# One core, four graph layers: the hand-written list of steps is replaced by another list

## The chip, the core and the metric

The kernel runs on one core of a Trainium2 chip. The metric is the device time in microseconds (us) of one execution, the median of three runs. The engines that matter are TensorE (PE; its weight loads are shown apart as PEld), VectorE (DVE), ScalarE (ACT), GpSimd (POOL), and SyncE (SP), which issues the DMAs. "L2252" is line 2252 of the kernel.

## The reference, cut to what matters

128 graphs of 64 nodes with 128 features each; `adj` holds edge weights, about a quarter of them nonzero. Four layers, each added to `x` after a layer norm and a ReLU:

```python
h = relu(layernorm(x))                       # layer 0: filters made from edge lengths
g = exp(coeff * (adj[..., None] - offsets) ** 2)             # 64 Gaussians an edge
Wf = (softplus(g @ W1.T + b1) - log 2) @ W2.T + b2           # a filter of 128 an edge
x = x + mlp(sum_j (h @ Wa.T)[j] * Wf[i, j] * adj[i, j] ** 2)  # mlp with softplus
h = relu(layernorm(x))                       # layer 1: hyperbolic attention
p = proj(mobius_add(mobius_matvec(W, h), expmap0(b)))
loc = logmap(p[i], p[j]);  self = logmap(p, p)
att = sigmoid(silu([self, loc] @ att_w1.T + att_b1) @ att_w2.T + att_b2)
s = sum_j att * loc * adj
u = silu([self, s] @ mlp_w1.T + mlp_b1) @ mlp_w2.T + mlp_b2 + self
x = x + proj(expmap0(silu(logmap0(proj(expmap(u, p))))))
h = relu(layernorm(x));  x = x + (d * adj * d) @ h @ W + b   # layer 2: degree norm
h = relu(layernorm(x));  x = x + [h, mean_message(h)] @ W_upd # layer 3
```

## The kernel before, in words

**Tiling.** `sparse_stack` does all the work that the given inputs need: 16 groups of 8 graphs. The partitions hold two graphs of 64 nodes, and a group is 4 such pairs (indices 0 to 3), so a node tile is 128 x (4 x 128). Work per edge goes only over edges that exist: each node's neighbours are sorted into slots, and the slots lie in three blocks c = 0, 1, 2 of 512, 494 and 208 columns a pair (`BLOCKS`, `WIDTHS`). A name such as `filter_of13` is block 1, pair 3; blocks 0 and 1 go by single pairs or by two (pairs 0-1 and 2-3, written 0 and 2), block 2 too.

**Streams.** The work of a group is written as generators, called streams. `load` brings x and adj (DMAs L1419 and L1420), `order` sorts the neighbours into one-hot tiles `oh` (L1533, on DVE), and `normed_x` makes layer 0's normed input (POOL L1470 and L1472, ACT L1478 and L1486). Layer 0's edges are done by four kinds:

- `weights_of` (DVE) spreads edge lengths over slots; `squares` (ACT L1588) squares them.
- `duo` (PE L1599, ACT L1604 and L1607) makes the Gaussians.
- `filter_of` has these steps: w1T matmul (PE L1621), Exp (ACT L1628), Ln (ACT L1631), w2T matmul (PE L1638), product (DVE L1643), and sums over slots (DVE L1401 and others).
- `neighbours` (PE L1679, ACT copy L1685) brings the neighbours' features, which L1643 also reads.

`layer1_nodes` does layer 1's node part, many tiny DVE, ACT and POOL operations; L1819 (ACT) and L1823 (DVE) are two of them, and `product_with_bias` (POOL L1805, then a DVE reduction) belongs to it. Layer 1's edges are done by `coefs_of` (DVE L1387 spreads; later L2076 merges the attention), `rows` (PE L2096, DVE L2099), `scores_of` (PE L2114 and L2118, ACT Silu L2123), `heads` (PE L2140, ACT Tanh L2146 into the tile `row`, then four DMAs L2151 that copy `row` into `th`) and `no_scores` (a POOL memset, L2157). `coefs_of`'s L2076 waits for these row copies. `rest1` ends layer 1; the steps needed here, by number, are:

- 8: the two hid matmuls L2217 and L2218; 9: Silu L2220
- 10 and 11: a matmul, and the add L2226, which makes u
- 12: squares of u, L1289 with four accumulator reads (ACT)
- 13: floor and power on POOL (L1279, L1275)
- 14: L2249 and L2250 (DVE); 15: Tanh L2252 (ACT); 16 and on: L2254, L2257 and more (DVE).

`product_with_h` (POOL L2234, DVE L2239) runs beside them. `rest2` is layers 2 and 3, ending with the output's DMA (L2421); L1256 is its product with adj, L2341 a POOL addition in it, and L2403 ACT scalings. L1242, L1249 and L1209 are helpers (matmul by pairs or by graph, PSUM copies).

**Order.** Each `yield on(engine, ...)` begins a step and names its engine, the buffer rings it takes, the events it needs, and where it matters the activation table ("log" or "silu") that ACT must have. The list `ORDER` (from line 775) fixes the order of all steps: a token `name@-4` runs the next step of that stream of group it-4, and `name@=2` runs a step of a stream that is there once (weights and constants) in iteration 2. The whole list is gone through for it = -6 to 21; one pass holds a step of every stage, for several groups at once. PE, DVE, ACT and POOL are under a manual schedule: each of them executes exactly in the order in which the list issues its instructions. SP's DMAs are issued by the steps that contain them. A step that names a table issues a table load if the last step in the list that named one named the other:

```python
        _, takes, _, table = s.want
        if table not in (None, self.table):
            self.table = table
            self.scalar.preload_act_table_set({"log": "natural_log_exp_and_others",
                                               "silu": "silu_and_others"}[table])
```

It is line 925. Steps on PE name tables too: `filter_of`'s first step (w1T matmul) names "log", and `rest1`'s step 8 (hid matmuls) and `scores_of`'s first step name "silu", so that the load is issued ahead of the activation that needs it:

```python
            yield on(PE, "big", "ex", table="log")      # filter_of, step 0
        yield on(PE, "sm", table="silu")                # rest1, step 8: hid matmuls
        yield on(ACT, table="silu")                     # rest1, step 9: act(hid, pt, AF.Silu, ...)
```

Of the kernel before, what the change touches and what calls it, by code (L numbers as in the profile page):

```python
# [772 lines left out]

PE, DVE, ACT, POOL = "PE", "DVE", "ACT", "POOL"
ORDER = """
scores_of03@-4 sum_of_both@-5 layer1_nodes@-3 turned_from5@=2 heads02@-4 rows12@-4 scores_of10@-4
scores_of11@-4 turned_from3@=-1 layer1_nodes@-3 rest1@-5 coefs_of00@-4 rest1@-5 rest1@-5
coefs_of20@-4 rest1@-5 order@-2 rest1@-5 layer1_nodes@-3 layer1_edges@-4 rest1@-5 order@-2
heads02@-4 layer1_nodes@-3 scores_of10@-4 scores_of11@-4 rest1@-5 coefs_of00@-4 rest1@-5 rows12@-4
rest1@-5 rest1@-5 order@-2 rest1@-5 order@-2 layer1_nodes@-3 coefs_of00@-4 rest1@-5 layer0@-2  # L780
rest1@-5 coefs_of02@-4 rest1@-5 rest1@-5 weights0@=-2 weights_of00@-2 rest1@-5 turned_from5@=2
rest1@-5 rest1@-5 coefs_of02@-4 scores_of12@-4 layer1_nodes@-3 heads10@-4 duo00@-2 scores_of13@-4
rest1@-5 rest1@-5 coefs_of00@-4 rest1@-5 coefs_of02@-4 rest1@-5 layer1_nodes@-3 rest1@-5 rest1@-5
layer1_nodes@-3 rest1@-5 turned_from3@=-1 sum_of_both@-5 coefs_of02@-4 weights_of02@-2
scores_of12@-4 heads10@-4 squares00@-2 duo00@-2 scores_of13@-4 weights1@=0 rest1@-5 rest1@-5
layer1_nodes@-3 rest1@-5 rows20@-4 rows22@-4 heads12@-4 heads12@-4 squares02@-2 rest1@-5 rows22@-4
layer1_nodes@-3 layer1_nodes@-3 rows20@-4 weights2@=2 coefs_of10@-4 rest1@-5 rest1@-5 rest1@-5
rest1@-5 rest2@-5 coefs_of10@-4 scores_of22@-4 layer1_nodes@-3 scores_of20@-4 scores_of22@-4
layer1_nodes@-3 norm_of_h1@-3 layer1_nodes@-3 duo02@-2 root_of_sums@-5 rest2@-5 layer1_nodes@-3
scores_of20@-4 layer1_nodes@-3 coefs_of12@-4 coefs_of10@-4 weights_of10@-2 coefs_of10@-4  # L790
weights_of12@-2 coefs_of12@-4 weights0@=1 layer1_nodes@-3 rest2@-5 coefs_of12@-4 weights_of20@-2
heads20@-4 heads20@-4 duo00@-2 rest2@-5 rest2@-5 weights2@=3 layer1_nodes@-3 duo02@-2 rest2@-5
rest2@-5 product_with_bias@-3 coefs_of12@-4 layer1_nodes@-3 coefs_of20@-4 turned_from0@=-4
filter_of00@-2 neighbours00@-2 filter_of01@-2 weights2@=2 layer1_nodes@-3 filter_of00@-2
filter_of00@-2 duo02@-2 neighbours00@-2 filter_of01@-2 layer1_edges@-4 coefs_of20@-4
layer1_nodes@-3 layer1_edges@-4 layer1_nodes@-3 layer1_edges@-4 layer1_nodes@-3 layer1_nodes@-3
rest1@-4 layer1_nodes@-3 layer1_nodes@-3 rest1@-4 layer1_nodes@-3 layer1_nodes@-3 rest1@-4
layer1_nodes@-3 neighbours01@-2 rest2@-5 filter_of02@-2 rest1@-4 filter_of00@-2 layer1_nodes@-3
neighbours01@-2 filter_of02@-2 squares10@-2 filter_of01@-2 filter_of02@-2 layer1_nodes@-3
product_with_bias@-3 layer0@-2 layer1_nodes@-3 layer1_nodes@-3 rest2@-5 layer1_nodes@-3  # L800
weights2@=2 layer1_nodes@-3 layer1_nodes@-3 layer1_nodes@-3 layer1_nodes@-3 order@-1
layer1_nodes@-3 rest1@-4 layer1_nodes@-3 layer1_nodes@-3 rest1@-4 layer1_nodes@-3 layer1_nodes@-3
rest2@-5 layer1_nodes@-3 layer1_nodes@-3 layer1_nodes@-3 layer1_nodes@-3 turned_from0@=-3
layer1_nodes@-3 layer1_nodes@-3 filter_of00@-2 layer1_nodes@-3 layer1_nodes@-3 layer1_nodes@-3
layer1_nodes@-3 layer1_nodes@-3 layer1_nodes@-3 layer1_nodes@-3 layer1_nodes@-3 norm_of_sum@-3
duo20@-2 neighbours02@-2 rest2@-5 filter_of01@-2 rest2@-5 filter_of00@-2 order@-1 weights2@=3
filter_of00@-2 filter_of01@-2 norm_of_sum@-3 rest2@-5 neighbours02@-2 duo20@-2 layer1_nodes@-3
duo20@-2 rest2@-5 norm_of_sum@-3 filter_of00@-2 layer1_nodes@-3 layer1_nodes@-3 layer1_nodes@-3
order@-1 rest2@-5 filter_of01@-2 filter_of03@-2 neighbours03@-2 turned_from1@=-4 rest1@-4
turned_from2@=-1 layer1_nodes@-3 weights0@=0 weights0@=1 filter_of03@-2 neighbours03@-2  # L810
squares20@-2 layer1_nodes@-3 filter_of03@-2 layer1_nodes@-3 rest1@-4 weights0@=-1 filter_of02@-2
norm_of_h@-3 x_self@-4 rest2@-5 filter_of02@-2 filter_of01@-2 norm_of_h@-3 turned_from2@=-1
filter_of01@-2 slots_ranks@=0 duo22@-2 layer1_nodes@-3 filter_of20@-2 neighbours20@-2 duo22@-2
layer1_nodes@-3 duo22@-2 filter_of20@-2 neighbours20@-2 layer1_nodes@-3 filter_of02@-2
layer1_nodes@-3 filter_of02@-2 filter_of02@-2 layer1_nodes@-3 weights0@=-1 filter_of20@-2
layer1_nodes@-3 filter_of22@-2 order@-1 weights0@=-1 attention@-3 filter_of03@-2 weights0@=1
order@-1 layer1_nodes@-3 order@-1 rest2@-5 layer1_nodes@-3 layer1_nodes@-3 order@-1
layer1_nodes@-3 filter_of03@-2 attention@-3 filter_of22@-2 layer1_nodes@-3 attention@-3
weights0@=-2 duo10@-2 order@-1 filter_of20@-2 neighbours22@-2 one_minus_z@-3 rest2@-5
one_minus_z@-3 slots_ranks@=-6 layer1_nodes@-3 one_minus_z@-3 one_minus_z@-3 filter_of03@-2  # L820
weights0@=-1 rest2@-5 rest2@-5 attention@-3 duo10@-2 layer1_nodes@-3 one_minus_z@-3 duo10@-2
rest2@-5 neighbours22@-2 order@-1 layer1_nodes@-3 filter_of20@-2 weights0@=0 layer1_nodes@-3
order@-1 layer1_nodes@-3 filter_of03@-2 layer1_nodes@-3 layer1_nodes@-3 filter_of03@-2
filter_of20@-2 layer1_nodes@-3 layer1_nodes@-3 layer1_nodes@-3 layer1_nodes@-3 layer1_nodes@-3
layer1_nodes@-3 layer1_nodes@-3 order@-1 weights0@=0 duo12@-2 filter_of10@-2 filter_of11@-2
weights2@=2 rest2@-5 order@-1 duo12@-2 filter_of10@-2 filter_of22@-2 rest2@-5 filter_of11@-2
filter_of10@-2 layer1_nodes@-3 neighbours10@-2 order@-1 filter_of22@-2 rest2@-5 filter_of10@-2
order@-1 neighbours10@-2 rest2@-5 rest2@-5 filter_of22@-2 weights2@=2 layer1_nodes@-3 order@-1
slots_ranks@=-2 filter_of22@-2 filter_of10@-2 duo12@-2 layer1_nodes@-3 filter_of11@-2 rest2@-5
rest2@-5 neighbours11@-2 filter_of12@-2 filter_of11@-2 order@-1 layer1_nodes@-3 layer1_nodes@-3  # L830
weights1@=-6 filter_of10@-2 layer1_nodes@-3 neighbours11@-2 filter_of12@-2 squares12@-2 rest2@-5
filter_of10@-2 layer1_nodes@-3 turned_from1@=-2 filter_of10@-2 layer1_edges@-3 coefs_of00@-3
filter_of10@-2 filter_of11@-2 order@-1 coefs_of02@-3 rest2@-5 filter_of11@-2 order@-1 order@-1
filter_of13@-2 neighbours13@-2 neighbours12@-2 rest2@-5 filter_of12@-2 filter_of13@-2
neighbours13@-2 neighbours12@-2 filter_of13@-2 rows00@-3 filter_of12@-2 turned_from4@=1
filter_of13@-2 rest1@-4 weights0@=1 weights2@=2 rest2@-5 rows00@-3 filter_of12@-2 filter_of11@-2
filter_of12@-2 filter_of11@-2 filter_of13@-2 filter_of12@-2 filter_of13@-2 filter_of12@-2
filter_of11@-2 filter_of13@-2 load@0 filter_of12@-2 rest1@-4 weights1@=-3 rows02@-3 rest1@-4
scores_of01@-3 scores_of00@-3 rest1@-4 filter_of13@-2 layer0@-2 rows02@-3 filter_of13@-2
weights0@=1 layer0@-2 normed_x@-1 rest1@-4 scores_of01@-3 scores_of00@-3 product_with_h@-4  # L840
rest1@-4 normed_x@-1 normed_x@-1 no_scores@-3 normed_x@-1 sums_of_columns@-1 product_with_h@-4
weights0@=-2 turned_from4@=1 coefs_of10@-3 product_with_h@-4 rest1@-4 order@-1 scores_of02@-3
heads00@-3 rows10@-3 normed_x@-1 scores_of03@-3 scores_of02@-3 rest1@-4 heads00@-3 normed_x@-1
rest1@-4 rest1@-4 rest1@-4 weights2@=2 rest1@-4 rest1@-4 rest1@-4 weights1@=1 rest1@-4 rest1@-4
rest1@-4 order@-1 rest1@-4 order@-1 rest1@-4 rest1@-4 rest1@-4 coefs_of12@-3 rows10@-3 rest1@-4
normed_x@-1 normed_x@-1
"""


def elements(ap):  # L850
    n = 1
    for d in ap.shape[1:]:
        n *= d
    return n


# [1617 lines left out]
```

## Time and profile before

| | us |
|---|---|
| median of the runs shown | 1792.26 (1792.07 to 1797.98) |
| the profiled execution's own time | 1792.99 |
| its span in the trace | 1791.2 |
| PE busy | 1558.6 (87%), 10231 matmuls |
| DVE busy | 1570.0 (88%), 5020 instructions |
| ACT busy | 1447.4 (81%), 2756 instructions |
| POOL busy | 422.6 (24%), 718 instructions |
| one ACT table load (L925), 64 of them | 1.283 |

Read it so: three engines are busy over 80% of the span, and the chain of waits (the page's fourth part) divides itself among them: PE 29%, ACT 29%, DVE 28%. The granted TensorE clock is 0.937 on average. The same stage comes again at equal distance: L2252 starts at 998.1, 1100.7, 1203.4 and 1306.0, so a period, one pass through the list, is 102.6 us, and about 13 such periods lie between the filling of the pipeline (to about 181) and its emptying (from about 1511).

### The profile page before, as it was taken

What the parts mean: (1) busy time and instruction counts of PE and PEld (TensorE: products, weight loads), DVE (VectorE), ACT (ScalarE), POOL (GpSimd) and SP (SyncE); (2) the same over time, 40 slices, a digit from 0 to 9 for tenths busy, and PEclk for the clock granted to TensorE, in tenths of its full rate; (3) what the DMA queues carried; (4) which work ended last, traced back from release to release, by engine and by line L of the source; (5) the groups of instructions that cost most, each with busy time, mean ns of one, the idle gap of its engine ahead of it and who ended that gap; (6) DMA issues with size and microseconds to landing.
All of it is one profiled execution on the core that took longest, in us unless ns stands there. A gap on an engine that the chain in (4) does not pass through costs nothing.

```text
span 1791.2 us, 30395 instructions
## 1 busy us (share of the span) xinstructions
PE 1558.6 (87%) x10231; PEld 848.9 (47%) x10231; DVE 1570.0 (88%) x5020; ACT 1447.4 (81%) x2756; POOL 422.6 (24%) x718
## 2 busy tenths in 40 slices
PE   3959898998989899898989899898989989896853
PEld 2424444544545454454545454454545445454442
DVE  5559899999999999999999989999999999987843
ACT  2858897979798897979899797979889797986632
POOL 2010213223221413223121322312141322302221
PEclk8979999999999999999999999999999999997965
DMA  2000202010110202011020201011020201102110
GB/s 62 6 1 7 57 7 54 10 45 22 27 45 16 57 7 56 16 33 33 16 57 10 63 7 44 22 28 45 16 57 1 56 11 30 33 13 51 39 30 9
DMA packets 57174, 53.64 MB, mean 30 GB/s; under 512 B 13616, under 2 KB 48816, under 8 KB 57008
## 3 DMA queue, kind: packets, MB, share of 16 engines
q1 hardware_dynamic: 57008, 51.60, 11.9%
q8 instruction: 83, 1.36, 0.3%
q14 instruction: 83, 0.68, 0.1%
HBM read 7.61 MB, written 4.19 MB: 7 GB/s over the span
## 4 chain that ended last, share of the span: by engine, by line
PE 29%; ACT 29%; DVE 28%; issue 5%; DMA 4%; POOL 3%; SPq 1%; DVEq 0%; ACTq 0%; POOLq 0%
PE big L1638 7%; PE sm L1242 6%; DVE ex L1643 4%; DMA th<-row 4%; PE big L1621 3%; PE big L1679 3%; ACT ex L1628 3%; DVE va L1387 3%; ACT ra L1685 2%; ACT e L1607 2%; ACT e L1604 2%; ACT ex L1631 2%; ACT v L1284 2%; PE sm L1249 2%; ACT n L1209 2%
## 5 line engine op out<-in xcount | busy, mean ns | idle before, releaser
L1638 PE MATMUL big<-ex,w2T 128*128 128x512 f32 (+2 forms) x768 | 295.2, 517 | 14.8 <-DVE den L1723 11.8
L1643 DVE SCALAR_TENSOR_TENSOR ex<-big,c_L_gnn_b,ra 128x1024 f32<-128x1024 f32 (+2 forms) x160 | 195.8, 1224 | 31.9 <-PE big L1638 31.2
L1621 PE MATMUL big<-e,w1T 64*128 64x512 f32 (+2 forms) x768 | 182.3, 572 | 15.9 <-ACT e L1607 8.0
L2114 PE MATMUL big<-va,U 64*128 64x512 f32 (+2 forms) x768 | 174.6, 530 | 19.4 <-DVE va L2099 19.3
L1638 PEld LDWEIGHTS big<-ex,w2T 128*128 128x128 f32 x768 | 134.3, 190 | 116.1 <-issue 75.5
L1628 ACT ACTIVATE ex<-big,c_L_gnn_b 128x1024 f32<-128x1024 f32 (+2 forms) x160 | 175.8, 1099 | 3.9 <-PE big L1621 1.8
L2123 ACT ACTIVATE ex<-big,c_L_gnn_att_b 128x1024 f32<-128x1024 f32 (+2 forms) x160 | 165.8, 1068 | 15.5 <-PE big L2118 10.7
L1679 PE MATMUL big<-va,a 64*128 64x512 f32 (+2 forms) x768 | 173.5, 551 | 3.8 <-ACT va L1588 1.6
L1685 ACT ACTIVATE ra<-big 128x1024 f32<-128x1024 f32 (+2 forms) x160 | 159.0, 1015 | 11.0 <-DVE den L1723 8.1
L1631 ACT ACTIVATE ex<-ex 128x1024 f32<-128x1024 f32 (+2 forms) x160 | 166.8, 1055 | 0.5
L2118 PE MATMUL big<-slot_r,Sx 64*128 64x512 f32 (+2 forms) x768 | 164.4, 502 | 0.0
L2234 POOL TENSOR_TENSOR w<-w,hh 128x512 f32<-128x512 f32 x16 | 20.6, 1287 | 592.8 <-DVE w L2226 578.4
L1401 DVE TENSOR_TENSOR ex<-ex 128x512 f32<-128x512 f32 (+3 forms) x256 | 121.2, 483 | 0.2
L2076 DVE COPY_PREDICATED att<-oh,th 128x256 f32<-128x256 uint16 (+1 forms) x256 | 109.3, 443 | 12.9 <-DMA th<-row 12.2
L2096 PE MATMUL big<-oh,pqs 64*64 64x512 bf16 (+2 forms) x1152 | 113.3, 333 | 0.0
L1621 PEld LDWEIGHTS big<-e,w1T 64*128 64x128 f32 x768 | 68.9, 203 | 87.6 <-issue 31.0
L2140 PE MATMUL sm<-ex,aw2b 128*32 128x512 f32 (+2 forms) x640 | 93.6, 583 | 12.5 <-ACT ex L2123 11.2
L2099 DVE COPY_PREDICATED va<-slot_r,big 128x1024 f32<-128x1024 uint32 (+2 forms) x96 | 102.2, 1066 | 1.6 <-PE big L2096 1.6
L1679 PEld LDWEIGHTS big<-va,a 64*128 64x128 f32 x768 | 69.7, 196 | 70.2 <-issue 31.1
L2118 PEld LDWEIGHTS big<-slot_r,Sx 64*128 64x128 f32 x768 | 73.9, 187 | 58.5 <-issue 58.5
L2114 PEld LDWEIGHTS big<-va,U 64*128 64x128 f32 x768 | 63.0, 185 | 69.1 <-DVE va L2099 38.2
L1256 PE MATMUL big<-adjT,v 64*128 64x64 f32 x256 | 31.5, 420 | 72.2 <-ACT v L1284 72.2
(571 smaller groups left out, 3717.0 us busy)
## 6 DMA issues: line engine op xcount, KB each, us to landing
th<-row SPq DMA_DIRECT2D x64, 256.0 KB, 3.5
th<-row SPq DMA_DIRECT2D x64, 247.0 KB, 3.4
th<-row SPq DMA_DIRECT2D x64, 104.0 KB, 2.3
x<-in_x_dram SPq DMA_DIRECT2D x16, 256.0 KB, 2.9
out_dram<-v SPq DMA_DIRECT2D x16, 256.0 KB, 2.3
adj<-in_adj_dram SPq DMA_DIRECT2D x16, 128.0 KB, 2.3
e<-in_L_gnn_att_w_dram SPq DMA_DIRECT2D x2, 64.0 KB, 4.2
bR<-in_L_gnn_mlp_w_dram SPq DMA_DIRECT2D x2, 64.0 KB, 3.2
```

Source lines behind the costliest of these rows:

```text
L1401: V.tensor_tensor(dst, a[:, :, 0:n], a[:, :, n:2 * n], ALU.add)
L1621: T.matmul(dst, lhsT=w1T[HALF[h], :], rhs=e[HALF[h], b, 0:W], start=True, stop=True)
L1628: act(ex[:, :, 0:wide], pre[:, :, 0:wide], AF.Exp, bias=b1)
L1631: act(ex[:, :, 0:wide], ex[:, :, 0:wide], AF.Ln, bias=1.0)
L1638: T.matmul(wf[:, b, cols], lhsT=w2T, rhs=ex[:, b if c < 2 else b ^ j, cols], start=True, stop=True)
L1643: V.scalar_tensor_tensor(ex[:, :, 0:wide] if c < 2 else two.rearrange("q (j r) -> q j r", j=2), wf[:, :, 0:wide], b2s, ra[:, :, 0:wide], A ...
L1679: T.matmul(nb[:, b, at * W:at * W + W], lhsT=rf[rows, p + j, :], rhs=factors[0][rows, k + j, :], start=True, stop=True)
L1685: act(ra[:, :, 0:wide], nb[:, :, 0:wide], AF.Copy)
L2096: T.matmul(rk[h, k, 0:W], lhsT=pqs[h, s, p, :], rhs=oh[h, p, at:at + W], start=s == 0, stop=s == 2)
L2114: T.matmul(pre[:, b, col], lhsT=U[h, p + k, :], rhs=coefs[h, k, :], start=True, stop=False)
L2118: T.matmul(pre[:, b, col], lhsT=Sx[s][h, p + k, :], rhs=slot_r[h, at:at + W], start=False, stop=s == 1)
L2123: act(a[:, :, 0:wide], pre[:, :, 0:wide], AF.Silu, bias=ab1)
```

## The change

Only the string `ORDER` is replaced; everything else of the kernel is the same. The new list begins about half a pass later in the cycle than the old one (so the offsets of the stages behind that point differ by one), and within the cycle many steps have changed places with their neighbours. `load` stands about half a pass later in relation to the rest. The same instructions are issued on PE, DVE (5020) and POOL (718), each in a somewhat different order, and SP's DMAs come in the same order, line by line. On ACT the activations are the same, and table loads are 92 where they were 64. Of the places that are spoken of below, the old and the new list (steps of one pass, step number after the dot, steps of no matter left out):

```
old: ... filter_of13.1 neighbours13.1 neighbours12.1 filter_of13.2 rows00.0 filter_of12.3 filter_of13.3 rest1.8 ...
new: ... rest1.8 rest2.30 filter_of13.0 neighbours12.0 neighbours13.0 filter_of13.1 filter_of12.2 neighbours12.1 filter_of13.2 ... rest1.9

old: rest1.14 order.19 scores_of02.0 heads00.0 rows10.0 normed_x.4 scores_of03.0 scores_of02.1 rest1.15 heads00.1 normed_x.5 rest1.16
new: order.18 order.19 rest2.31 filter_of11.6 rows00.1 ... rest1.14 scores_of02.0 heads00.0 scores_of03.0 normed_x.4 rows10.0 rest1.15 heads00.1 normed_x.5 rest1.16 ... scores_of02.1 scores_of03.1

old: no_scores between normed_x.2 (L1470) and normed_x.3 (L1472);  new: ahead of product_with_h.0 (L2234)
old: coefs_of00's first merge (L2076) behind rest1.30;              new: behind rest1.33
old: product_with_bias.0 (L1805) behind rest2.6 (L2341);            new: ahead of it
```

The lines of the diff in which these stand:

```diff
 ORDER = """
...
-filter_of13@-2 neighbours13@-2 neighbours12@-2 rest2@-5 filter_of12@-2 filter_of13@-2
-neighbours13@-2 neighbours12@-2 filter_of13@-2 rows00@-3 filter_of12@-2 turned_from4@=1
-filter_of13@-2 rest1@-4 weights0@=1 weights2@=2 rest2@-5 rows00@-3 filter_of12@-2 filter_of11@-2
...
-rest1@-4 normed_x@-1 normed_x@-1 no_scores@-3 normed_x@-1 sums_of_columns@-1 product_with_h@-4
-weights0@=-2 turned_from4@=1 coefs_of10@-3 product_with_h@-4 rest1@-4 order@-1 scores_of02@-3
-heads00@-3 rows10@-3 normed_x@-1 scores_of03@-3 scores_of02@-3 rest1@-4 heads00@-3 normed_x@-1
...
+coefs_of00@-3 rest2@-5 filter_of11@-2 filter_of10@-2 rest1@-4 rest2@-5 filter_of13@-2
+neighbours12@-2 neighbours13@-2 filter_of13@-2 filter_of12@-2 neighbours12@-2 filter_of13@-2
+neighbours13@-2 rows00@-3 filter_of12@-2 filter_of13@-2 filter_of11@-2 order@-1 weights2@=2
+layer0@-2 coefs_of02@-3 order@-1 order@-1 rest2@-5 filter_of11@-2 rows00@-3 filter_of12@-2
...
+layer0@-2 normed_x@-1 rest1@-4 scores_of00@-3 scores_of01@-3 no_scores@-3 product_with_h@-4
+rest1@-4 normed_x@-1 normed_x@-1 normed_x@-1 product_with_h@-4 coefs_of10@-3 product_with_h@-4
+rest1@-4 scores_of02@-3 turned_from4@=1 heads00@-3 turned_from0@=-4 turned_from1@=-3
+scores_of03@-3 normed_x@-1 rows10@-3 rest1@-4 heads00@-3 normed_x@-1 rest1@-4 rest1@-4 rest1@-4
...
```

## The prediction

> **What bounds the kernel now.** The chain of waits of the whole run names no engine (PE 29%, ACT 29%, DVE 28%), so I cut one period at the places where the limit changes hands. The first view is busy time by windows (columns: window, length, busy us and count of PE, PEld, DVE, ACT, POOL, then clock, DMA share, GB/s):
>
> ```profile
> 283.00:1511.00 1228.00, 1138.65 (x7658) 618.95 (x7654) 1157.05 (x3706) 1079.47 (x2065) 314.54 (x516) 0.97 0.13 31
> 1074.60:1100.80 26.20, 26.09 (x153) 12.94 (x153) 26.06 (x55) 17.38 (x30) 6.57 (x9) 1.00 0.06 16
> 1100.80:1177.20 76.40, 68.23 (x491) 38.53 (x488) 70.17 (x256) 72.52 (x144) 19.77 (x35) 0.96 0.15 37
> ```
>
> The period of 102.6 us has two parts. For 26.2 us (from filter_of10's w2T matmul to L2252) PE and DVE are full and ACT has 8.8 us to spare. For 76.4 us ACT is the fullest, 72.5. So the first part is set by PE and DVE, the second mostly by ACT; work added to an engine in its own part costs, in the other part it does not.
>
> The second view is what ACT waited for in 283 to 1511, about 12 periods (us in total, times, longest); then the same for DVE:
>
> ```profile
> ACT w L2220 <- PE sm L2218: 44.3, 12, 3.7
> ACT w L1289 <- DVE w L2226: 32.7, 12, 2.7
> ACT a L1486 <- POOL d_n L1705: 15.7, 12, 1.3
> ACT ra L1685 <- DVE den L1723: 8.1, 12, 1.0
> ```
>
> ```profile
> DVE ex L1643 <- PE big L1638: 13.9, 24, 0.7
> DVE s L1823 <- ACT nn L1819: 12.0, 12, 1.1
> DVE e L1963 <- ACT gr L1209: 8.2, 12, 0.7
> DVE att L2076 <- DMA th<-row: 6.3, 12, 1.3
> ```
>
> ACT's two long waits (3.7 and 2.7 a period) lie in the first part, where it has slack. L1486 (1.31 a period) and L1685 (0.68) lie in the second, where they lengthen the period. Row copies cost DVE 6.3 us in 12 periods, 0.5 in each: all that a better guess at landing times could win directly. L1486 really waits for a matmul's result and L1685 for PE's buffer, which DVE's L1643 frees; the POOL and DVE rows named had long been done.
>
> The third view is the timeline where the first part ends (start, length, engine, line), of ACT, DVE and POOL:
>
> ```profile
> 1085.57 1.28 ACT L925 ACT_TABLE_LOAD   x1
> 1090.54 0.69 ACT L2220 ACTIVATE w<-sm,c_L_gnn_mlp_b 128x512 f32<-128x512 f32 x1 [3.69 <-PE sm L2218]
> 1095.14 3.20 ACT L2123 ACTIVATE ex<-big,c_L_gnn_att_b 128x1024 f32<-128x1024 f32 x3
> 1100.73 0.20 ACT L2252 ACTIVATE k__11817<-rb 128x4 f32<-128x4 f32 x1 [2.39 <-DVE rb L2249]
> ```
>
> ```profile
> 1099.16 0.17 DVE L2239 RECIPROCAL rb<-rb 128x4 f32<-128x4 f32 x1
> 1099.42 1.28 DVE L2249 TENSOR_TENSOR rb<-rb,un 128x4 f32<-128x4 f32 x1
> 1100.62 0.17 DVE L2250 RECIPROCAL ur<-un 128x4 f32<-128x4 f32 x1
> 1100.71 0.35 DVE L1533 TENSOR_TENSOR oh<-pos,slot_k 128x440 bf16<-128x440 bf16 x1
> ```
>
> ```profile
> 1097.91 1.07 POOL L1470 TENSOR_TENSOR a<-xp,o_mv 128x512 f32<-128x512 f32 x1
> 1098.93 0.52 POOL L2157 MEMSET att<- 128x512 f32 x1
> 1099.41 1.27 POOL L1472 TENSOR_TENSOR xp<-xp,r_L_gnn_bd 128x512 f32<-128x512 f32 x1
> ```
>
> L2249 does 512 numbers, as its neighbours of 0.17 do, yet is on record for 1.28: it ends (1100.70) when POOL's L1472 ends (1100.68). The Trainium skill, "SBUF — State Buffer", section "Who interferes with whom", has this as a port that the two engines share and that the first to issue holds for its whole instruction; the trace agrees (0.163 at the shortest, 1.275 in the median of this line's 16).
>
> **The change, part by part.** One period, in us; a plus is longer.
>
> *Table loads.* 92 for 64, two more in each steady pass: hid's matmul step (silu) now comes before filter_of13's first step (log), hid's Silu after it, so ACT loads silu, log and silu. Two loads of 1.283 are 2.57. They fall into the first part, where ACT idles 3.69 ahead of L2220. In exchange hid's matmuls no longer come last: PE has them 8.65 us of matmuls earlier, and L2220 then waits for its own third load, not for PE. ACT's last Ln before it ended at 1085.56; with 2.57 more and the third load it would be free at about 1089.4, before L2220's present 1090.54. Value 0. If the cover goes (ACT late for w2T of filter_of12 or filter_of13, where I find 2.3 spare: 1.41 from Ln's end at 1085.56 to the matmul at 1086.97, plus the 1.72 of PE work now ahead of it, less 0.83 of ACT shift), it costs at most 0.3. One place for the skill: "ScalarE: Activation LUTs", section "What ACT_TABLE_LOAD costs", gives a drain of about 1.38 us on top of each load of 1.283. The trace does not show one: Ln ends at 1085.55 and the load starts at 1085.57; another ends at 1130.96 and L1607 starts at 1130.98. By the page the two loads would be 5.3, an estimate.
>
> *ACT's second part.* From L2252 to filter_of10's Ln ACT's own work grows from 70.76 to 72.13, +1.37: scores_of02's Silu (1.10, one of the three at 1095.14) moves behind L2252, and a copy of `order` (0.27). But that Silu and scores_of03's, 2.1 together, now stand ahead of L1486, whose wait of 1.31 is for something else: −1.31. And DVE has 0.71 less to do from L1823 to filter_of00's L1643, because product_with_bias's reduction (0.59) is now done inside the wait at L1823, so the buffer that L1685 waits for comes free sooner: −0.68. Sum −0.62. Bounds: nothing swallowed, +1.37; all swallowed and the 0.27 hidden, −0.89.
>
> *The row copies.* coefs_of00's L2076 gets 1.54 us of DVE work put ahead of it, and its 0.5 goes. But that DVE time lies in ACT's part: what is late next is L1823, which waits for ACT's L1819 (1.0 a period) and will wait longer by as much. Value 0, bounds 0 and −0.5.
>
> *DVE's first part.* order's piece of 440 (L1533, 0.35, of which 0.28 does not overlap) covered DVE's wait for L2252; it moves into the full part, and DVE also gets more instructions that read what the one just before wrote (50 for 46 a period; such a pair costs about 0.12 more than an independent one, by the starts at 1101.17, 1101.25 and 1101.44). I put 0.28 and 0.12 here, +0.40; L2254 will then wait 0.2 for L2252. Bounds 0 and +0.76 (all four pairs).
>
> *POOL.* no_scores' memset (0.52; 0.48 from start to start) no longer stands between L1470 and L1472, so L1472 ends up to 0.48 earlier and with it L2249: −0.48. Bounds: 0, if POOL gets there later by as much, to −0.48; and +0.2, if L1470 and L1472 back to back hold up the second L1387 of coefs_of10 that runs beside them.
>
> *SP, load, the rest.* SP has the same DMAs in the same order, so `load`, half a pass later in the list, costs nothing (the loads land in 2.3 to 2.9 us). PE's work is the same, 95.29 a period.
>
> *Ends.* At the start DVE's first instruction is now L1143, which waits for a weight to land at about 8.9, where it did 3.9 us of constants before: between 0 and +3.9; I take +1, as most of DVE's first 283 us are waits (65 in all). The emptying I take as unchanged.
>
> *Sum.* −0.62 + 0.40 − 0.48 = −0.70 a period; times 13, −9.1; with the start −8. The profiled execution took 1792.99 (0.7 over the median): 1785.
>
> **The rivals.**
>
> *More of DVE's waits go.* DVE idles 4.4 us a period: L1643, L1823, L1963, L2076 and others. The whole list was reordered, and I followed only its larger moves. If half goes, −2.2 a period, times 13 is −29: 1764; all of it would be 1736. For it: the waits are many and small (0.5 to 1.1). Against it: L1823's and L1963's are for ACT, which does not get faster in its part.
>
> *The added work lands, the waits stay: slower.* The 1.31 and 0.68 belong to the arrival of PE's and DVE's results. If these come later by what was put ahead of ACT (PE's L1242 for L1486 waits in its queue behind matmuls that need ACT's output), ACT waits again behind the added Silu, and nothing is swallowed. It decides at L1486: if its idle time is still over 0.7, the case holds. Then +1.37 + 0.40 = +1.77 a period, times 13 is +23: 1816. For it: PE is full in the first part, and its 3.8 us wait for L1284 and 1.4 for L2099 show that it follows ACT and DVE closely.
>
> *The table switch costs more than its row.* A load that also keeps ACT from starting for another of its own length (1.28; the row shows 0.02) puts 2.6 more ahead of L2220, which then starts about 1.4 later than now and moves L2226, POOL's power and L2249. About 0.4 of it fits before the stall of L2249 ends, so +1.0 a period on top of the forecast, +13: 1798. The ScalarE page's drain, named above, is this case; the rows speak against it.
>
> *The list does not do what it says.* The waits for row copies are 0.5 of 102.6, and the rest may only change places: 1792.
>
> **How the numbers follow.** What a measurement of this kernel tells from no change is about 0.5%, 9 us: 1783.3 to 1801.2.
>
> - Forecast 1785, own range 1776 to 1794: 0.40 (faster 0.15, same 0.24, slower 0.01).
> - More waits go, 1764: 0.23, all faster.
> - Added work lands, 1816: 0.26 (slower 0.23, same 0.03).
> - Table switch, 1798: 0.03 (same 0.02, slower 0.01).
> - No effect, 1792: 0.08 (same 0.05, slower 0.03).
>
> Faster 0.38, same 0.34, slower 0.28. The range goes from 1758 to 1818: it takes in both large rivals' middles and leaves out their far ends, 0.08 below and 0.12 above.
>
> **What would show it.** L2252's starts give the period: 101.9 if the sum is right, 104.4 for the slower rival, 100.4 for the faster. Table loads: 92 in the row of L925, and L2220's idle of 3.69 gone. ACT's part: the idle ahead of L1486 and L1685 gone; if over 0.7 is left at L1486, that term fails. L2076's wait near 0 and L1823's longer: otherwise the row copies did pay. L1472 directly behind L1470 and L2249 near 0.8: if it is 1.28 again, POOL's term fails. The forecast is wrong as a whole if the two windows change by more than 1 each, or if the time is lost before 181 or after 1511.

## The result, and the profile after

| | before | after |
|---|---|---|
| median, us (22 runs each) | 1792.99 | 1790.57 |
| ratio to before | | 0.9984, 95% interval 0.9978 to 0.9991 |
| span of the profiled execution | 1791.2 | 1787.7 |
| first start of L2252 | 282.3 | 282.3 |
| from there to the thirteenth start (12 periods) | 1228.4 | 1227.3 |
| from there to the end | 280.5 | 278.1 |

The change is real but small: 0.16%, some 2.9 us, where 8 were forecast. In the two traces (3.5 us apart) the start is the same, twelve periods bring 1.1 and the emptying 2.4. Ten of the twelve periods are between 101.9 and 102.3 (102.1 in the mean; the same ten of before 102.3), but two are 103.4.

The windows of the changed kernel, whole steady part and the two parts of one period (columns as above):

```profile
283.00:1511.00 1228.00, 1142.54 (x7665) 621.00 (x7661) 1178.48 (x3715) 1109.38 (x2091) 308.19 (x516) 0.97 0.13 31
1101.70:1177.90 76.20, 69.36 (x500) 39.12 (x500) 72.49 (x259) 74.13 (x145) 19.22 (x36) 0.96 0.16 37
1177.90:1203.60 25.70, 25.70 (x143) 12.31 (x143) 25.53 (x53) 18.29 (x30) 6.08 (x7) 1.00 0.06 16
```

DVE is busy 21 us longer than before (1178.5 for 1157.1) with the same instructions: 1.8 a period, where the prediction had 0.12, and at most 0.5, for dependent pairs. In the second part (76 us) it went from 70.2 to 72.5. The waits of ACT and of DVE in the same stretch:

```profile
ACT w L1289 <- DVE w L2226: 44.5, 12, 3.7
ACT ra L1685 <- DVE den L1723: 6.0, 11, 1.1
ACT ex L1628 <- PE big L1621: 5.5, 12, 0.5
ACT e L1321 <- DVE e L1967: 4.7, 11, 0.4
```

```profile
DVE ex L1643 <- PE big L1638: 21.1, 12, 1.8
DVE att L2076 <- DMA th<-row: 1.8, 2, 1.0
```

What the prediction saw in the list has come: L2220's 3.7 and L1486's 1.3 are gone, and DVE waits for row copies in two periods only. L1685's idle time has not gone: with its smaller rows it is 9.1 us in all, for 8.1 before. New are ACT's waits at L1628, in the part where ACT has time to spare, and at L1321 for DVE, in ACT's own part: something made DVE late there. The timeline of DVE and then of POOL shows it:

```profile
1153.61 0.13 DVE L2376 TENSOR_SCALAR ind<-sums 128x4 f32<-128x4 f32 x1
1153.65 1.25 DVE L2377 TENSOR_SCALAR rdeg<-sums 128x4 f32<-128x4 f32 x1
1154.82 0.41 DVE L1401 TENSOR_TENSOR ex<-ex 128x256 f32<-128x256 f32 x1
```

```profile
1152.04 1.49 POOL L2184 TENSOR_TENSOR w<-hh,cs 128x512 f32<-128x512 f32 x1
1153.61 1.27 POOL L2185 TENSOR_TENSOR w<-w,r_L_gnn_mlp_b 128x512 f32<-128x512 f32 x1
```

L2377 works on four numbers a partition, like L2376 before it, and takes 1.25: it ends when POOL's L2185 ends (x_self, the step that adds the self term to u). Such a lengthening beside a POOL operation is called a hold below. In before L2377 starts 5 us after the end of L2185 and takes 0.16. A second new hold is that of weights_of20's L1391, in most periods the third of its five, 1.48 for 0.37, beside POOL's L1805 (product_with_bias), which the new list also moved. These two lines add 13 us each to DVE's busy time in 283 to 1511; L2249 and L1823, which are held for less than before, take 6 off.

The last view is the one that the prediction did without: the chain of waits within some periods of the steady part, not of the whole run. Of before (690 to 895) and of after (590 to 795), a few of its pieces:

```profile
698.04 0.52 SPq L2151
698.62 3.57 DMA th<-row
702.28 0.45 DVE att L2076
```

```profile
618.70 1.97 PE big L1256 x16
620.67 3.52 PE big L1621 x8
...
640.52 1.16 DVE rdeg L2377
642.00 1.20 DVE ex L1643
...
659.89 1.67 PE big L1638 x8
...
676.54 3.63 PE big L1638 x8
```

Before, a period's chain runs in the full part over DVE to L2249, L2252, row's Tanh, the row copy (of coefs_of02 here) and L2076. After, it stays on PE for 44 us from filter_of22's w2T matmul (659.89), goes by ACT and POOL to L1256, by PE to L2201, then 17 us over DVE, L2377 among it, then over ACT. The reading from here on is that there are two chains of nearly one length, that the new list took the first away, and that on the second it put 1.1 us. The experiments test it.

### The profile page after: what moved, and what is told of

Read it like the earlier page. It is cut to its first block, busy times and chain, and to the rows that moved or that the text cites. A ratio compares the mean times of both kernels' runs of the same rounds, so it can differ in the third digit from the quotient of the medians.

```text
span 1787.7 us, 30380 instructions
## 1 busy us (share of the span) xinstructions
PE 1563.6 (87%) x10231; PEld 853.9 (48%) x10231; DVE 1591.2 (89%) x5020; ACT 1480.6 (83%) x2784; POOL 414.4 (23%) x718
## 4 chain that ended last, share of the span: by engine, by line
PE 45%; DVE 26%; ACT 21%; POOL 3%; issue 2%; DMA 1%; SPq 0%; DVEq 0%; ACTq 0%; POOLq 0%
PE big L1638 8%; PE sm L1242 7%; PE big L2114 5%; PE big L2096 5%; PE big L1621 4%; DVE ex L1643 3%; PE big L1679 3%; PE sm L2140 3%; PE big L2118 3%; DVE ex L1401 2%; ACT e L1604 2%; ACT ex L1628 2%; PE sm L1249 2%; ACT ex L1631 2%; DVE va L1387 1%
## 5 line engine op out<-in xcount | busy, mean ns | idle before, releaser
L1638 PE MATMUL big<-ex,w2T 128*128 128x512 f32 (+2 forms) x768 | 291.3, 514 | 10.6 <-ACT ex L1628 8.1
L1643 DVE SCALAR_TENSOR_TENSOR ex<-big,c_L_gnn_b,ra 128x1024 f32<-128x1024 f32 (+2 forms) x160 | 195.7, 1223 | 47.0 <-PE big L1638 44.1
L1621 PE MATMUL big<-e,w1T 64*128 64x512 f32 (+2 forms) x768 | 191.0, 600 | 20.7 <-ACT e L1607 19.2
L1628 ACT ACTIVATE ex<-big,c_L_gnn_b 128x1024 f32<-128x1024 f32 (+2 forms) x160 | 171.1, 1084 | 11.7 <-PE big L1621 8.0
L1685 ACT ACTIVATE ra<-big 128x1024 f32<-128x1024 f32 (+2 forms) x160 | 157.9, 987 | 10.5 <-DVE den L1723 6.5
L1679 PE MATMUL big<-va,a 64*128 64x512 f32 (+2 forms) x768 | 163.8, 524 | 1.2 <-ACT ra L1685 1.2
L2076 DVE COPY_PREDICATED att<-oh,th 128x256 f32<-128x256 uint16 (+1 forms) x256 | 108.7, 440 | 5.9 <-DMA th<-row 5.7
L2099 DVE COPY_PREDICATED va<-slot_r,big 128x1024 f32<-128x1024 uint32 (+2 forms) x96 | 102.0, 1064 | 4.3 <-PE big L2096 4.3
L1256 PE MATMUL big<-adjT,v 64*128 64x64 f32 x256 | 31.5, 424 | 72.8 <-ACT v L1284 72.8
```

The lines of the kernel that those rows point to most:

```text
L1621: T.matmul(dst, lhsT=w1T[HALF[h], :], rhs=e[HALF[h], b, 0:W], start=True, stop=True)
L1628: act(ex[:, :, 0:wide], pre[:, :, 0:wide], AF.Exp, bias=b1)
L1638: T.matmul(wf[:, b, cols], lhsT=w2T, rhs=ex[:, b if c < 2 else b ^ j, cols], start=True, stop=True)
L1643: V.scalar_tensor_tensor(ex[:, :, 0:wide] if c < 2 else two.rearrange("q (j r) -> q j r", j=2), wf[:, :, 0:wide], b2s, ra[:, :, 0:wide], A ...
L1679: T.matmul(nb[:, b, at * W:at * W + W], lhsT=rf[rows, p + j, :], rhs=factors[0][rows, k + j, :], start=True, stop=True)
L1685: act(ra[:, :, 0:wide], nb[:, :, 0:wide], AF.Copy)
```

## The experiments

All were run for five rounds beside the kernel before on the same chip; a ratio is to that. Chips differ between experiments, so these are compared with each other and with the changed kernel by their ratios. Edits of the list are shown by step.

**The hold at L1391.** The first theory, called P, was that the port holds ate the gain.

```diff
-coefs_of12.1 coefs_of10.4 coefs_of12.2 weights_of20.0 layer1_nodes.16
+weights_of20.0 coefs_of12.1 coefs_of10.4 coefs_of12.2 layer1_nodes.16
```

> The changed kernel with one step moved: weights_of20 (five L1391 on DVE) goes ahead of coefs_of12's first merge (L2076), so that its third L1391 no longer runs beside POOL's L1805. Theory P (the port: what the forecast missed is that the new list puts short DVE operations beside POOL's operations of 1.27 us, and DVE is held until these end; 1.1 us a period at L1391, 1.1 at L2377): the L1391 row is back from 1.48 to 0.4, coefs_of12's L2076 does not wait for its row copy in any period, ACT's waits for DVE (L1321 0.41, L1685) shrink, the period falls by 0.4 to 1.1, the time by 5 to 14 us against the changed kernel. Rival W (ACT's own added work sets its part, DVE's stalls are hidden in it): DVE only waits 1.1 longer at filter_of22's L1643 (1.76 now), and the time stays within 2 us, but for the two longer periods (2.6 us) if they go.

Ratio 0.9978 (0.9969 to 0.9986): 1.1 us better than the changed kernel, which the intervals do not tell apart. The hold did not go, it went to the next in line: the L2076 that now runs beside L1805 (coefs_of12's second) takes 1.50 instead of 0.44. So this was no test of P. The two periods of 103.4 did go (all twelve are 102.0 to 102.4), but the others rose from 101.9 to 102.3.

**The table loads, taken back in the changed kernel.**

```diff
-rest1.8 rest2.30 filter_of13.0 ... filter_of13.3 filter_of11.5
+rest2.30 filter_of13.0 ... filter_of13.3 rest1.8 filter_of11.5
```

> The changed kernel with rest1's hid matmul step put back behind filter_of13's w2T matmul: 64 table loads again, and L2220 waits for PE again. If the prediction's step holds (two loads more lie in ACT's idle time, value 0): the steady period stays within 0.3, the time within 4 us, and the emptying, where hid's matmuls then come late, gets 1 to 2.5 us longer. If the added table loads are what ate the gain: the period is shorter by 0.5 to 1, the time by 6 to 13.

Ratio 0.9994 (0.9986 to 1.0003), 1.8 us worse than with the loads, with intervals that overlap. The steady period is the same within 0.1 (its ten shorter ones 102.1 in the mean) and the three last periods are 0.9 longer. In the changed kernel two loads more a period cost nothing.

**One part alone: L1805 first.**

```diff
-rest2.5 rest2.6 product_with_bias.0
+rest2.5 product_with_bias.0 rest2.6
```

> The kernel before with one part of the change alone: product_with_bias's POOL step (L1805) ahead of rest2's L2341. By the prediction's step, L1823's wait swallows DVE's reduction and L1685's 0.68 a period goes: -0.7 a period, about -9 us. By theory P L1805 then runs beside DVE's weights_of20 or whatever stands there and holds it for up to 1.1, and what is won is lost again: within 4 us of before, with a DVE row near 1.3 to 1.5 that was 0.2 to 0.4.

Ratio 1.0018 (1.0010 to 1.0027): 3.3 us slower than before. The edit does less than the expectation says: it moves the POOL step alone, and DVE's reduction (L1261) stays 5.8 us behind L1823, where in the changed kernel it stands directly ahead of it. L1823's wait does shrink, from 1.07 to 0.18 in the median, but the timeline of DVE and POOL shows another reason:

```profile
1126.10 2.47 DVE L1387 TENSOR_TENSOR va<-oh,adjT 128x768 f32<-128x768 bf16 x2
```

```profile
1127.06 1.26 POOL L1805 TENSOR_TENSOR n<-n,r_L_gnn_b_lin 128x512 f32<-128x512 f32 x1
```

The same two instructions are 1.37 together in before. The second is now held for 1.1 ahead of L1823, and L1823's wait takes up 0.9 of it. So the run shows what L1805's new neighbour costs, 0.3 a period; the prediction's −0.68 it does not test.

**One part alone: hid's matmul step first, with the 28 loads.**

```diff
-filter_of13.0 neighbours13.0 ... filter_of13.3 rest1.8
+rest1.8 filter_of13.0 neighbours13.0 ... filter_of13.3
```

> The kernel before with one part alone: rest1's hid matmul step ahead of filter_of13's first step, as in the changed kernel; 92 table loads, L2220 no longer waits for PE. By the prediction's step: nothing in the steady period (within 0.3), since DVE and PE set that part; the emptying gets 1 to 2.5 us shorter, as it did in the changed kernel. If a table switch costs more than its row: the period is longer by 1, the time by 13.

Ratio 1.0069 (1.0057 to 1.0081): 12.4 us slower, the rival's number. Its mechanism does not show: here too the loads start 0.02 us after the instruction before and most are followed after 0.01. DVE's waits show where it begins:

```profile
DVE ex L1643 <- PE big L1638: 21.3, 36, 0.7
```

24 waits have become 36. The new twelve, 0.62 each, are filter_of12's L1643: its Ln comes behind the loads, its w2T matmul behind the Ln. The prediction had found 2.3 spare there; there is none. These waits are 7 of the 12 us.

**The hold at L2377 taken off.** Theory C is that of the two chains.

```diff
-            G.tensor_tensor(u, hh, bl(st["cs"], D), ALU.mult)
-            G.tensor_tensor(u, u, bm(mb2, NP), ALU.add)
+            G.memset(u, 0.0)
+            G.memset(u, 0.0)
```

> The changed kernel, with x_self's two POOL operations (L2184, L2185, which add the self term to u) replaced by two fills of the same tile, so that nothing of POOL reads SBUF there; the self term is left out. Theory C (the chain of one period, as the trace of the changed kernel shows it: 43 us of PE without a gap from filter_of22's w2T matmul on, then ACT, POOL and PE to L1256 and L2201, then 16 us of DVE in which L2377 is held for 1.1 by L2185, then ACT): L2377 is short again and the 1.1 comes off the chain; the period falls by 0.4 to 1.1, the time by 5 to 14 us against the changed kernel. If the shortfall lies elsewhere: the period stays within 0.2, since DVE then waits as much longer at filter_of22's L1643.

Ratio 0.9944 (0.9931 to 0.9956): 7 us faster than the changed kernel, most periods 101.3 to 101.6. L2377's row (shortest, median, longest in ns) in before, in the changed kernel and in this run:

```profile
L2377 DVE TENSOR_SCALAR rdeg<-sums x16: 160/161/165, 341.4 to 1773.2; 128x4 f32<-128x4 f32 x16
L2377 DVE TENSOR_SCALAR rdeg<-sums x16: 157/1266/1292, 334.3 to 1769.8; 128x4 f32<-128x4 f32 x16
L2377 DVE TENSOR_SCALAR rdeg<-sums x16: 156/161/385, 334.5 to 1762.7; 128x4 f32<-128x4 f32 x16
```

ACT's wait at L1321 is gone, as theory C has it. Of the 1.1 the period gets 0.5 back; then the chain runs another way, from L2292 over DVE. The edit also frees POOL sooner, but in the steady part of the changed kernel the only wait put down to POOL is L2292's, and that is the same in this run (5.6 us in 12 periods). The same edit in the kernel before is the control:

> The control to the run that took x_self's operations off POOL's read port: the same edit in the kernel before (x_self's L2184 and L2185 are fills, the self term is left out). There L2377 stands twelve steps later and is not held. Theory C: nothing is gained, the time within 3 us of before. If less work on POOL helps in general (its other holds of DVE, or its results earlier): 5 to 10 us less, as in the changed kernel.

Ratio 0.9998 (0.9989 to 1.0006): nothing. So it is the hold that the new list made, and not less work on POOL as such.

**A version that keeps the work.** x_self on DVE, in DVE's wait at filter_of22's L1643 (its step moves in the list too, to just ahead of filter_of22.4):

```diff
         def x_self():
-            yield on(POOL)
-            G.tensor_tensor(u, hh, bl(st["cs"], D), ALU.mult)
-            G.tensor_tensor(u, u, bm(mb2, NP), ALU.add)
+            yield on(DVE)
+            V.tensor_tensor(u, hh, bl(st["cs"], D), ALU.mult)
+            V.tensor_tensor(u, u, bm(mb2, NP), ALU.add)
```

> The changed kernel with x_self's two operations moved from POOL to DVE, just ahead of filter_of22's L1643, where DVE waits 1.76 for PE. Theory C: L2377 is short again (1.1 off the chain), and x_self's 1.3 us of DVE lie in the wait that is there; period -0.3 to -1.1, time 4 to 14 us less than the changed kernel, about 1777 to 1787. If DVE's own work sets the period: 1.3 more of it, less 1.1, so no change or up to 3 us more.

Ratio 0.9950 (0.9937 to 0.9963), 6 us faster than the changed kernel. L2377 is at 0.16, and the wait at filter_of22's L1643 fell from 1.76 to 0.61: x_self's 1.3 went into it. With `weights_of20` moved as in the first experiment as well:

> The changed kernel with x_self on DVE ahead of filter_of22's L1643, and with weights_of20 ahead of coefs_of12's first merge. Theory C: L2377's hold is off the chain (period 101.4), and the row copy that lands 1 us late in groups 7 and 8 meets an L2076 that comes 1.5 later, so that the two periods of 103 fall to 101.4 too: 2 to 3.5 us less than x_self on DVE alone, about 1780. Rival: the hold by L1805 moves to L2076 and puts the period back to 102.3; then 1785 to 1790.

Ratio 0.9928 (0.9915 to 0.9940), median 1780.46, the fastest of all, though its interval just overlaps that of the run before. DVE waits for row copies in no steady period, and the two long periods fall from 103.1 and 102.8 to 102.2 and 102.0, less far than expected.

**Four terms of the forecast, each alone.** The row copies, in the kernel before:

```diff
-rest1.30 coefs_of00.1 rest1.31 rest1.32 coefs_of20.0 rest1.33
+rest1.30 rest1.31 rest1.32 coefs_of20.0 rest1.33 coefs_of00.1
```

> The kernel before with one part alone: coefs_of00's first merge (L2076) behind rest1.33, as in the changed kernel, so that it comes 1.5 us of DVE work after where it waited for its row copy. By the prediction's step: value 0, the time within 3 us of before. Theory C (in the kernel before the chain of a period runs from L2252 over row's Tanh, the row copy's 3.6 us and L2076 into DVE): the wait comes off the chain, 0.3 in most periods and 1.1 in the three long ones, so 4 to 8 us less than before.

Ratio 0.9996 (0.9987 to 1.0005). The prediction's 0 holds and theory C's 4 to 8 us do not. Both had misread where the wait was: in before coefs_of00's merge waits in three groups only (9 to 11 counted from 0, 1.0 to 1.3 each, and those three periods do fall by 0.4), and the 0.2 of most periods is at coefs_of02's first merge. There the edit makes the wait 0.1 shorter, and the period stays at 102.3: its chain now runs over PE, as in the changed kernel, and DVE waits for PE at rest2's L1299 in ten of these periods (3.1 us in all), for six (1.8) in before.

The one-hot piece, put back in the changed kernel:

```diff
-order.18 order.19 rest2.31 ... rest1.14 scores_of02.0 ... heads00.0
+order.18 rest2.31 ... rest1.14 scores_of02.0 ... heads00.0 ... order.19 rest1.15
```

> The changed kernel with order's one-hot piece of 440 (L1533) put back between L2250 and the wait for L2252. By the prediction's step (+0.40 for moving it into the full part): the period falls by 0.3 to 0.4, the time by 4 to 5 us. Theory C: DVE is not on the chain there, PE is; the period stays within 0.1, the time within 2 us.

Ratio 0.9986 (0.9977 to 0.9995), as the changed kernel. L2254's wait of 0.18 for L2252 goes, and a wait of 0.27 for PE comes at filter_of12's L1643: in the full part L1533 had been cover for the loads (work that DVE does in place of a wait), not a cost.

The fill on POOL, in the kernel before:

```diff
-product_with_h.0 rest1.13 normed_x.1 normed_x.2 no_scores.0 normed_x.3
+no_scores.0 product_with_h.0 rest1.13 normed_x.1 normed_x.2 normed_x.3
```

> The kernel before with one part alone: no_scores' fill ahead of product_with_h on POOL, no longer between L1470 and L1472. By the prediction's step: L2249's hold gets 0.3 to 0.48 shorter and the period with it, 4 to 6 us less. Theory C (two chains of nearly the same length, and L2249 lies on only one of them): the hold gets shorter, the time stays within 2 us.

Ratio 0.9999 (0.9990 to 1.0007), though L2249's median fell from 1.275 to 0.954 (0.968 in the changed kernel):

```profile
L2249 DVE TENSOR_TENSOR rb<-rb,un x16: 162/954/958, 281.0 to 1744.0; 128x4 f32<-128x4 f32 x16
```

The hold is 0.3 shorter and the period is not. DVE's waits for PE at L1299, before and here, show where the 0.3 goes: DVE comes earlier and waits 0.36 a period longer for the other chain.

```profile
DVE v L1299 <- PE sm L1242: 1.8, 6, 0.4
DVE v L1299 <- PE sm L1242: 6.1, 10, 0.8
```

The Silu, in the kernel before:

```diff
-scores_of03.0 scores_of02.1 rest1.15 ... normed_x.6 normed_x.7 scores_of03.1
+scores_of03.0 rest1.15 ... normed_x.6 normed_x.7 scores_of02.1 scores_of03.1
```

> The kernel before with one part alone: scores_of02's Silu behind L2252, ahead of scores_of03's, so that both stand ahead of L1486. By the prediction's step: L1486's wait of 1.31 swallows the 1.10, so -0.2 a period, 3 us less than before. The slower rival of the prediction: L1486 keeps over 0.7 of its wait and the period is up to 1.1 longer, up to 14 us more. Theory C: L1486's wait goes, and the time stays within 2 us.

Ratio 1.0070 (1.0058 to 1.0083), 12.5 us slower. The edit does not do what the expectation says: L1486 (normed_x.7) stays ahead of both Silus, and its wait stays:

```profile
ACT a L1486 <- POOL d_n L1705: 15.7, 12, 1.3
```

So this is the price of the moved Silu where nothing covers it: about 1.0 a period. With both ahead of L1486:

```diff
-scores_of03.0 scores_of02.1 rest1.15 ... normed_x.6 normed_x.7 scores_of03.1
+scores_of03.0 rest1.15 ... normed_x.6 scores_of02.1 scores_of03.1 normed_x.7
```

> The kernel before with scores_of02's and scores_of03's Silu both ahead of L1486 on ACT, as in the changed kernel; the run before this one had only moved scores_of02's Silu behind L2252, with L1486 still ahead of both, and its wait of 1.31 stayed. By the prediction's step: L1486's wait is swallowed (-1.31) and pays for the 1.10; the time is within 4 us of before, and 9 to 13 us less than the run with the one Silu. The prediction's slower rival: the wait at L1486 comes back behind the two, and the time stays near 1805.

Ratio 1.0003 (0.9994 to 1.0012). L1486's wait is swallowed and pays for the Silu; the rest of 0.2 does not arrive.

**Why the loads cost in one kernel and not in the other.** On top of hid's step first, the cover:

```diff
-rest2.31 rows00.1 filter_of12.4 filter_of11.6
+order.19 rest2.31 filter_of11.6 rows00.1 filter_of12.4
```

> The kernel before with hid's matmul step first (92 loads, which alone cost 13 us, with a new wait of 0.62 at filter_of12's L1643), and in addition order's L1533 of 440 and filter_of11's L1660 put ahead of that L1643, as in the changed kernel. Theory F (the two loads make filter_of12's Ln late by 0.6 to 0.7 and the new list covers that with other DVE work, 0.40 and 0.28): the new wait goes, and the time is within 4 us of before. If the loads cost by themselves: near 1805 still.

Ratio 1.0059 (1.0046 to 1.0073): the wait at filter_of12 is gone, but only some 2 of the 12.4 us come back, so theory F explains little. What is left shows at coefs_of00's L2076, which waits up to 1.7 for a row copy in late groups. With the later merge as well (the edit shown above for the row copies), and with the merge but no cover:

> The kernel before with three parts of the change: hid's matmul step first (92 loads), L1533 and L1660 as cover ahead of filter_of12's L1643 (with which it took 1802), and coefs_of00's first merge (L2076) behind rest1.33. Theory G (the kernel before has no room left on the chain over the row copies: the little that the loads and L1533 add arrives at L2076, above all in the groups whose copies land 1 us late; the later merge gives that room): the periods of 104 go, the time is 6 to 10 us less than without the merge, 1792 to 1796. If the loads themselves cost: still near 1802.

> The same without the cover: hid's matmul step first, and the later merge, in the kernel before. Theory G: 1793 to 1799, so the merge is the larger part of what makes the loads free, and the cover ahead of filter_of12's L1643 (0.62 of wait) is worth up to 3 us. If the loads themselves cost: near 1805.

Ratios 1.0040 (1.0027 to 1.0054) and 1.0056 (1.0042 to 1.0069). By the ratios (1.0069 bare, 1.0059 and 1.0056 with one of them, 1.0040 with both) cover and merge are worth about 2 us each and 5 together; the interval with both is apart from that of neither, the single steps' are not. Both times theory G had expected are missed, and some 7 of the 12.4 us are not explained: why the loads cost nothing in the changed kernel stays open for the larger part.

## Why the prediction was wrong, step by step

- **The sum.** −0.70 a period was forecast, and it is −0.1 over all twelve, −0.3 in the ten without a late copy. Two steps failed. The first is a cost that the sum does not have: the new list puts x_self's L2185 beside L2377, which is held for 1.1 on the chain, and without this hold the changed kernel is 7 us faster (0.5 a period; two runs, with a control that gains nothing). The second is the adding up itself: it took the period as 26.2 us of one limit and 76.4 of another, and put the terms of both parts together. The chains of single periods show two closed paths of nearly one length, and L2249's hold, made 0.3 shorter alone, only lengthened a wait: a term counts only if it shortens the longer path. That the paths are nearly equal is read from the chains and from that run; no run measures the length of each.
- **ACT's part, −0.62.** Its mechanism was right in the main: L1486 swallows the Silu (two experiments, 12 us apart). Of L1685 it was not, as its idle time in all did not shrink (9.1 us for 8.1). In the fifth period DVE's second L1643 starts 47.0 after L2252, for 47.9 in before, so 0.9 is won by there. At the third nothing is left of it (53.8 in both): between them stands L2377 with its hold, a cost that the step did not have. With the hold off the third starts at 52.6. The prediction had seen such holds (L2249) and looked for them only where an instruction was already held; beyond L1387, which it named as a bound, it did not ask which DVE and POOL instructions the new list would put side by side.
- **Luck.** Without the hold the period is 0.6 shorter than before's, close to the forecast's 0.70. That the other two terms do not spoil this is luck: POOL's −0.48 and DVE's +0.40 nearly cancel in the sum, and POOL's change and the moved piece came to 0 each when tried alone.
- **POOL, −0.48.** L2249 did get 0.3 shorter; nothing came of it.
- **DVE, +0.40.** No cost for the moved piece (0.28 of it): it covers a wait that the loads would open. The 0.12 for dependent pairs was not tried alone.
- **Table loads, 0.** Right in the changed kernel; the 2.3 us of room were wrong: in the kernel before the loads alone cost 12, and with cover and merge still 7.
- **Row copies, 0.** The value was right when tried alone, the reading under it was not: of the 6.3 us only 3.5 were coefs_of00's, in three groups. L1823, which was to wait longer, does not wait at all. Not foreseen was that coefs_of12's copies come 1 us late in groups 7 and 8 and that DVE, displaced, then meets more holds (L1391 and L1387, one after the other): two periods, some 1.3 each.
- **More of DVE's waits go, the faster rival.** Its condition nearly came true: DVE's waits in 283 to 1511 fell from 49 us (4.1 a period, where the prediction had 4.4) to 26, by 1.9 a period. Its price did not, because the holds filled the room: DVE's busy time rose by 21.
- **The ends.** The start is +0 for +1; the emptying is −2.4, where one of the thirteen periods, −0.7, was counted in. There hid's earlier matmuls do help: in the last two whole stages L2220's wait falls from 2.6 to 0.6 and from 3.5 to 2.1, and with hid's step put back the last three periods were 0.9 longer.
- **The table switch as a rival.** The load and its neighbour in the changed kernel:

```profile
1191.44 1.28 ACT L925 ACT_TABLE_LOAD   x1
1192.73 0.69 ACT L2220 ACTIVATE w<-sm,c_L_gnn_mlp_b 128x512 f32<-128x512 f32 x1
```

The gap is 0.01. The drain of 1.38 us that the Trainium skill ("ScalarE: Activation LUTs", section "What ACT_TABLE_LOAD costs") adds to each load would be 39 us of ACT in 28 loads, an estimate from the page's figure; no trace here shows it, and taking the loads out did not make the changed kernel faster.

## What to carry to other kernels

Before summing what a reordering moves, follow the chain of waits through a few periods of the steady state, and look for a second chain of nearly the same length; what shortens only one of them can be worth nothing by itself. When instructions change neighbours, list for each POOL operation that reads SBUF which DVE instructions will now run beside it: here one of four numbers a partition was held for 1.1 us and cost 0.5 a period. Spare time next to a move is a claim of its own; test the move alone, since cover can come from another move of the same change.

## What the hardware showed that was not expected

A TENSOR_SCALAR of 128x4 with a single input (L2377) is held by a POOL operation for 1.1, a COPY_PREDICATED (L2076) for 1.06, and TENSOR_TENSORs of bf16 (L1387, L1391) for 1.1. "SBUF — State Buffer", section "Who interferes with whom", of the Trainium skill says that a DVE instruction with one SBUF input contends only in a mode that uses two ports, and names tensor_scalar among those that can enter it; the trace agrees so far that L2377, a tensor_scalar with one SBUF input, is held (1.25 for 0.16), but does not show its mode. The section does not name a predicated copy, though its rule for two SBUF inputs would cover L2076, which reads `oh` and `th`; the run with `weights_of20` moved shows one held (1.50 for 0.44). Beside POOL operations of the same kind (L2184, L2341), BATCH_NORM_STATS2 (L1269, 0.28) and TENSOR_REDUCE (L1261, 0.67) keep their length.

The late row copies are not chance: coefs_of12's L2076 waits 0.8 to 1.0 in groups 7 and 8, and in no other steady group, in the changed kernel and in the four runs of it with hid's step put back, the one-hot piece put back, or x_self changed. In before it waits 1.1 in group 7, and coefs_of00's 1.0 to 1.3 in groups 9 to 11. Why they land late just there the runs do not show.
